# The bonus term of an RWKV-6 recurrence: from a unit of its own on VectorE to a tile made on GpSimd

## The chip, the cores and the metric

The kernel runs on one core of a Trainium2 chip. The metric is the device time in microseconds (us) of one execution, the median of several runs. Engines are named as in the profile: PE is TensorE (PEld its weight loads), DVE is VectorE, ACT is ScalarE, POOL is GpSimd, SP is SyncE, which only issues DMAs here. All data are float32.

## The reference

One RWKV-6 block on `x` of 32 sequences, 128 tokens, 512 channels (32 heads of 16). A layernorm and a token shift give five mixed inputs; four products give `r`, `k`, `v` and the gate, a small two-layer product gives the decay `w`. Then, per sequence and head, a state of 16 x 16 runs over the tokens:

```
def step(s, rkvw):
    r_t, k_t, v_t, w_t = rkvw
    a = k_t[:, :, :, None] * v_t[:, :, None, :]
    out = jnp.einsum('bhk,bhkd->bhd', r_t, u * a + s)
    return (a + w_t[:, :, :, None] * s, out)
```

The term with `u` is the bonus: the token's own `k` and `v`, weighted by `u`, which the state does not hold yet. Its sum over the 16 key channels is one number per token and head, `rk = sum_q r_q u_q k_q`, times `v`. After the recurrence come a norm per head, the gate, a product with `Wo` and the residual, then a second layernorm with a channel-mixing part (three products) and a second residual.

## The kernel before

**Groups and lanes.** The sequences are taken in NG = 8 groups of 4. In the recurrence the 128 partitions are the 4 x 32 pairs of sequence and head; `r`, `k`, `v`, `w` are tiles of 128 x 16 channels x 128 tokens, brought into this layout by DMAs (`to_lanes`).

**Tokens in pairs.** The state is computed for every second token only. `prep` (L567) multiplies neighbouring decays into `w01`, folds the decay of the second token into `k` and that of the first into `r`, and `bonus` (L627) makes two small tiles for a group: `rk` (128 x 128 tokens) and `a10` (128 x 64 pairs), the latter holding what the first token of a pair gives to the second.

**Units.** The recurrence of a group runs in two halves `dh` of 8 value channels (DH = 8), each with 16 units `q`, one per key channel (S = 16), and one more unit for the bonus. A unit goes through the engines so:

- POOL (`rec_pool`): product `am` = v x k_q (L704, 128 x 1024), then the sum of each pair into `a` (L708, 128 x 504). ACT puts the initial state into the first column of `a` (L690) and a copy of `w01` into the PSUM tile `sc` (L679).
- DVE (`rec_dve`): a scan of `sc` with `a` (L726), which runs all 64 pair steps of 8 channels in one instruction, and the product with r_q into `rm` (L728, 128 x 1024).
- PE (`rec_pe`): 8 transposes of `rm` with the permutation `by_head`, accumulated over all units in the PSUM tile `acc` (L761). After the last unit ACT copies `acc` into `y` (`rec_out`, L775).

The unit q = 16 has no scan. DVE makes `rm` = v x rk (L735), then v of the first tokens x a10 into a PSUM tile (L738), and adds that to the second tokens of `rm` (L742). PE transposes it like the others, as the 17th and last term of `acc`.

**Buffers.** `am` has 1, `a` 2, `rm` 2, `sc` 2, `acc` 1, `w01` 1, `v`, `r` and `k` 2 each, `blk` (128 x 512 in SBUF, which also takes projections on their way out) 4, `ps` (PSUM) 4, `y` 1.

**The other work.** `front_mix`, `front_proj` and `front_gate` make the inputs of later groups (products at L391 and L410; in groups after the first, part of the mixing adds are on POOL, L467), `layernorm_T` has a small power on POOL (L352). `back` does all that follows the recurrence (products at L849, L391, L923, L939). For the last group, `back` runs in two halves of two sequences, `last1` and `last2`.

**Order.** Each engine runs its instructions in the order in which the program emits them. That order is made by a small planner (`Plan`): every part of the work is a generator that yields `Op`s with an engine, an assumed duration, the buffers that it reads, writes, allocates and ends. `Plan.start` works out when an operation could start; among those that could start within `EPSILON` us of the earliest, `pick` takes the one with the smallest due value. Due values run linearly from v0 to v1 over the steps of a generator, in units of groups, from the table `DUE`. A generator whose `need` is not met, or whose buffers are all open, is passed over. So a change of EPSILON, of DUE, or of any Op can move every instruction of every engine, and with them the DMA issues on the SP and ACT queues.

Of the kernel before, what the change touches and what calls it, by code (L numbers as in the profile page):

```python
# [11 lines left out]
ALU = mybir.AluOpType  # L12
AX = mybir.AxisListType

P = 128
B, L, E = 32, 128, 512
H, S = 32, 16
# [3 lines left out]
NG = B // GB  # L21
N = GB * L
T2 = L // 2
DH = 8
# [11 lines left out]
PE, DVE, ACT, POOL, SP = range(5)  # L36
# [6 lines left out]
LANDING = 2.0  # L43
HOP = (0.2, 0.05, 0.05, 0.04, 0.08)
ON_POOL = (2, 3, 4)
EPSILON = 0.0388


DUE = {"rec": (0.171, 1.108), "mix": (-4.67, -2.417), "proj": (-4.683, 4.311), "gate": (0.588, 0.608), "prep": (-4.19, 1.684), "back": (-0.012, 3.928), "last1": (-21.388, 9.796), "last2": (10.392, 13.665)}


class Buf:
# [20 lines left out]
class Plan:  # L73
# [103 lines left out]
    def pick(self, best):  # L177
        t0 = min(t for t, _ in best)
        return min((x for x in best if x[0] <= t0 + EPSILON), key=lambda x: x[1][3] + x[1][4] * x[1][2])


@with_exitstack
def rwkv6_block(ctx: ExitStack, tc: tile.TileContext, x, prev, s0, vecs, u, maa_w1, maa_w2,
# [11 lines left out]
    nc = tc.nc  # L195
# [84 lines left out]
    def pair(ap):  # L280
        return ap.rearrange("p c (n j) -> p c n j", j=2)
# [386 lines left out]
    unit = {}  # L668
# [25 lines left out]
    def rec_pool(gs):  # L694

        for g in gs:
            d = data[g]
            yield Op(POOL, 0.0, need=lambda: "w01" in d and ("v", "all") in d)
            k, v = d["k"], d["v"]
            for dh in range(NDH):  # L700
                ds = slice(dh * DH, (dh + 1) * DH)
                for q in range(S):
                    (am,) = yield Op(POOL, 2.39, r=[(k, None), (v, None)], w=[(0, None)], alloc=["am"], port=True)
                    nc.gpsimd.tensor_tensor(am.t, v[:, ds, :], k[:, q : q + 1, :].to_broadcast([P, DH, L]), ALU.mult)  # L704
                    yield Op(POOL, 0.0, need=lambda: (g, dh, q, "a") in unit)
                    a, am2 = unit[g, dh, q, "a"], pair(am.t)
                    yield Op(POOL, 1.03, r=[(am, None)], w=[(a, 1)], port=True, end=[am])
                    nc.gpsimd.tensor_tensor(a[:, :, 1:T2], am2[:, :, 0 : T2 - 1, 0], am2[:, :, 0 : T2 - 1, 1], ALU.add)  # L708
                    unit[g, dh, q, "sum"] = True
            k.open = False  # L710

    def rec_dve(gs):

        for g in gs:
            d = data[g]
            yield Op(DVE, 0.0, need=lambda: "w01" in d and ("v", "all") in d)
            r, v = d["r"], d["v"]
            r2, v2 = pair(r.t), pair(v.t)
            for dh in range(NDH):
                ds = slice(dh * DH, (dh + 1) * DH)  # L720
                for q in range(S):
                    yield Op(DVE, 0.0, need=lambda: (g, dh, q, "sum") in unit and (g, dh, q, "sc") in unit)
                    a, sc = unit[g, dh, q, "a"], unit[g, dh, q, "sc"]
                    yield Op(DVE, 1.22, r=[(a, None)], w=[(sc, None)], end=[a])
                    scf = sc.t.rearrange("p d n -> p (d n)")
                    nc.vector.tensor_tensor_scan(scf, scf, a.t.rearrange("p d n -> p (d n)"), 0.0, ALU.mult, ALU.add)  # L726
                    (rm,) = yield Op(DVE, 1.21, r=[(sc, None), (r, None)], w=[(0, None)], alloc=["rm"], end=[sc])
                    nc.vector.tensor_tensor(  # L728
                        pair(rm.t), sc.t.unsqueeze(3).to_broadcast([P, DH, T2, 2]),
                        r2[:, q : q + 1, :, :].to_broadcast([P, DH, T2, 2]), ALU.mult)  # L730
                    unit[g, dh, q, "rm"] = rm
                q = S
                yield Op(DVE, 0.0, need=lambda: "a10" in d)
                (rm,) = yield Op(DVE, 1.2, r=[(v, None), (d["rk"], None)], w=[(0, None)], alloc=["rm"], port=True)
                nc.vector.tensor_tensor(rm.t, v[:, ds, :], d["rk"].t.unsqueeze(1).to_broadcast([P, DH, L]), ALU.mult)  # L735
                (am,) = yield Op(DVE, 0.67, r=[(v, None), (d["a10"], None)], w=[(0, None)], alloc=["ps"], port=True)
                bo = am.t.rearrange("p (d n) -> p d n", n=T2)
                nc.vector.tensor_tensor(bo, v2[:, ds, :, 0], d["a10"].t.unsqueeze(1).to_broadcast([P, DH, T2]),  # L738
                                        ALU.mult)
                yield Op(DVE, 0.67, r=[(am, None)], w=[(rm, None)], end=[am])  # L740
                rm2 = pair(rm.t)
                nc.vector.tensor_tensor(rm2[:, :, :, 1], rm2[:, :, :, 1], bo, ALU.add)  # L742
                unit[g, dh, q, "rm"] = rm
            r.open = v.open = d["rk"].open = d["a10"].open = False

    def rec_pe(gs):

        for g in gs:
            d = data[g]
            for dh in range(NDH):  # L750
                acc = None
                for q in range(S + 1):
                    yield Op(PE, 0.0, need=lambda: (g, dh, q, "rm") in unit)
                    rm = unit[g, dh, q, "rm"]
                    if acc is None:
                        (acc,) = yield Op(PE, 0.875, r=[(rm, None)], w=[(0, None)], alloc=["acc"], end=[rm])
                    else:
                        yield Op(PE, 0.875, r=[(rm, None)], w=[(acc, None)], end=[rm])
                    for i in range(DH):

                        nc.tensor.matmul(acc[:, i, :], lhsT=rm[:, i, :], rhs=by_head, is_transpose=True,  # L761
                                         start=(q == 0 and i % 4 == 0), stop=(q == S), skip_group_check=True)
                unit[g, dh, "acc"] = acc

    def rec_out(gs):
# [181 lines left out]
    for gen, n in ((rec_dve, 2), (rec_pool, 3), (rec_act, 1), (rec_state, 1), (rec_pe, 2), (rec_out, 0.1)):  # L947
        v0, v1 = DUE["rec"]
        plan.add(gen(range(NG)), v0, NG - 1 + v1, n * NU * NG)
    for g in range(NG):  # L950
        for gen, name, n in ((front_mix, "mix", 40), (front_proj, "proj", 72), (front_gate, "gate", 17),
                             (prep, "prep", 40), (back, "back", 140)):
            v0, v1 = DUE[name]
            if name != "back" or g < NG - 1:
# [4 lines left out]
    for bs, name in (((0, 1), "last1"), ((2, 3), "last2")):  # L959
        v0, v1 = DUE[name]  # L960
        plan.add(back(NG - 1, data[-1], bs, W), NG - 1 + v0, NG - 1 + v1, 130)
# [38 lines left out]
```

## Time and profile before

| | |
|---|---|
| median of 3 runs | 1536.72 us (1534.43 to 1536.81) |
| the profiled execution | 1535.0 us, of which the span from the first to the last instruction is 1533.2 us |
| mean granted PE clock | 0.959 |
| PE | 5344 matmul passes, busy 1410.0 us |
| DVE | 1618 instructions, busy 1270.9 us |
| ACT | 1277 instructions, busy 656.2 us |
| POOL | 632 instructions, busy 1024.8 us |
| DMA | 146.88 MB |

A float32 product of 512 columns shows as two passes, so 16 products of 128 x 128 x 512 are 32 entries. The busy time of a group of instructions is the union of their spans; the mean duration of a matmul is longer than its share of that union, since one begins before the one before it has drained. A line "A <- B" among the waits says that engine A was idle in front of its instruction until B released it.

### The profile page before, as it was taken

The numbers are of one execution on the slowest core, as the hardware profiler recorded it, in microseconds if no ns is written. First come the engines' busy times: TensorE is split into PE (matmuls) and PEld (weight loads), VectorE is DVE, ScalarE is ACT, GpSimd is POOL, SyncE is SP. The second block draws the span as 40 slices with busy tenths as digits, with TensorE's granted clock in tenths as the row PEclk, the third lists the DMA queues.
The fourth block names the chain that finished last, engine by engine and source line by source line (L and its number), as shares of the span: only waits on it lengthen the run. The fifth ranks groups of instructions, "written<-read, shape, count | busy, mean of one in ns | idle before, by whom it ended". The sixth has DMA issues, their size and how long they took to land.

```text
span 1533.2 us, 16578 instructions
## 1 busy us (share of the span) xinstructions
PE 1410.0 (92%) x5344; PEld 746.6 (49%) x5344; DVE 1270.9 (83%) x1618; ACT 656.2 (43%) x1277; POOL 1024.8 (67%) x632
## 2 busy tenths in 40 slices
PE   3997898899999999999999999999999998778788
PEld 1343454455554555455554555455544555455444
DVE  5537789989998899899988899899988898878732
ACT  4233242423743356323743365424733354344242
POOL 3014893877787859687786959686777959678400
PEclk9798899899999999999999999999999999889879
DMA  6120331244304431244304521343305421400220
GB/s 223 42 84 23 104 108 29 78 132 145 117 11 144 144 131 43 79 133 142 117 29 134 183 92 35 97 140 124 110 32 163 126 89 41 159 27 28 93 71 28
DMA packets 127559, 146.88 MB, mean 96 GB/s; under 512 B 8176, under 2 KB 77296, under 8 KB 126448
## 3 DMA queue, kind: packets, MB, share of 16 engines
q1 hardware_dynamic: 92112, 128.81, 25.6%
q10 hardware_dynamic: 35360, 17.02, 3.9%
q8 instruction: 42, 0.69, 0.2%
q14 instruction: 45, 0.37, 0.1%
HBM read 94.41 MB, written 17.83 MB: 73 GB/s over the span
## 4 chain that ended last, share of the span: by engine, by line
PE 51%; DVE 27%; POOL 13%; issue 6%; DMA 2%; ACT 1%; SPq 1%; DVEq 0%; POOLq 0%; ACTq 0%
PE ps L391 18%; PE acc L761 8%; POOL am L704 7%; PE ps L939 6%; PE ps L923 6%; PE ps L410 6%; DVE sc L726 5%; POOL a L708 4%; DVE rm L728 4%; PE ps L849 2%; DVE rk L642 2%; DVE ps L634 2%; PE ps L397 2%; PE ps L444 2%; DVE ps L470 1%
## 5 line engine op out<-in xcount | busy, mean ns | idle before, releaser
L704 POOL TENSOR_TENSOR am<-v,k 128x1024 f32<-128x1024 f32 x256 | 610.3, 2384 | 88.7 <-DMA r<-blk 70.4
L391 PE MATMUL ps<-mx,wt 128*128 128x512 f32 (+1 forms) x1312 | 583.2, 593 | 8.8 <-DVE mx L472 3.4
L708 POOL TENSOR_TENSOR a<-am 128x504 f32<-128x504 f32 x256 | 286.1, 1118 | 201.5 <-DVE sc L726 181.1
L391 PEld LDWEIGHTS ps<-mx,wt 128*128 128x128 f32 x1312 | 244.3, 194 | 276.2 <-issue 259.1
L728 DVE TENSOR_TENSOR rm<-sc,r 128x1024 f32<-128x1024 f32 x256 | 312.9, 1222 | 38.3 <-PE acc L761 22.9
L726 DVE TENSOR_TENSOR_SCAN sc<-sc,a 128x512 f32<-128x512 f32 x256 | 313.4, 1224 | 32.7 <-POOL a L708 30.5
L761 PE MATMUL acc<-by_head,rm 128*128 128x128 f32 x2176 | 290.8, 283 | 36.0 <-DVE rm L728 29.9
L761 PEld LDWEIGHTS acc<-by_head,rm 128*128 128x128 f32 x2176 | 252.3, 146 | 135.9 <-issue 54.4
L679 ACT COPY sc<-w 128x512 f32<-128x512 f32 x256 | 151.4, 591 | 219.5 <-DVE rm L728 197.0
L690 ACT COPY a<-st 128x8 f32<-128x8 f32 x256 | 52.2, 204 | 180.1 <-DVE sc L726 156.4
L467 POOL TENSOR_TENSOR mx<-mx,xnT 128x512 f32<-128x512 f32 x84 | 99.7, 1198 | 40.9 <-DVE mx L465 40.3
L923 PE MATMUL ps<-wt,mx 128*128 128x512 f32 x256 | 115.7, 595 | 0.0
L540 ACT COPY blk<-ps 128x512 f32<-128x512 f32 x96 | 56.0, 584 | 137.6 <-PE ps L391 137.6
L849 PE MATMUL ps<-wt,mx 128*128 128x512 f32 x256 | 112.8, 598 | 0.6 <-DVE rk L642 0.6
L410 PE MATMUL ps<-tha,w2p 64*128 64x512 f32 x256 | 89.1, 677 | 18.0 <-DVE mx L472 12.0
L939 PE MATMUL ps<-wt,ev 128*128 128x512 f32 x224 | 102.4, 600 | 2.7 <-DVE mx L472 2.7
L352 POOL TENSOR_TENSOR rstd<-rstd,mhalf 128x4 f32<-128x4 f32 (+1 forms) x17 | 20.2, 1191 | 120.1 <-DVE rstd L350 120.1
L470 DVE SCALAR_TENSOR_TENSOR ps<-ps,vec,sx 128x512 f32<-128x512 f32 x76 | 57.3, 753 | 36.7 <-PE ps L410 36.3
L465 DVE SCALAR_TENSOR_TENSOR mx<-ps,vec,sx 128x512 f32<-128x512 f32 x84 | 61.8, 743 | 21.8 <-PE ps L410 21.7
L849 PEld LDWEIGHTS ps<-wt,mx 128*128 128x128 f32 x256 | 48.9, 192 | 62.5 <-issue 56.5
L923 PEld LDWEIGHTS ps<-wt,mx 128*128 128x128 f32 x256 | 46.4, 190 | 51.0 <-issue 46.8
L939 PEld LDWEIGHTS ps<-wt,ev 128*128 128x128 f32 x224 | 40.9, 192 | 45.3 <-issue 39.9
(108 smaller groups left out, 1341.1 us busy)
## 6 DMA issues: line engine op xcount, KB each, us to landing
x<-in_x SPq DMA_DIRECT2D x15, 1024.0 KB
wt<-in_wk SPq DMA_DIRECT2D x8, 1024.0 KB
wt<-in_wr SPq DMA_DIRECT2D x8, 1024.0 KB
wt<-in_wg SPq DMA_DIRECT2D x8, 1024.0 KB
dgate<-blk SPq DMA_DIRECT2D x32, 256.0 KB
wt<-in_wo SPq DMA_DIRECT2D x8, 1024.0 KB
wt<-in_fk SPq DMA_DIRECT2D x8, 1024.0 KB
wt<-in_fr SPq DMA_DIRECT2D x8, 1024.0 KB
```

The source lines that it names most:

```text
L391: nc.tensor.matmul(p, lhsT=w[:, c, e * P : (e + 1) * P], rhs=xin[:, c, cols], start=(c == 0), stop=(c == NE - 1))
L410: nc.tensor.matmul(p.t, lhsT=w[h, :], rhs=t[h, :], start=True, stop=True)
L467: nc.gpsimd.tensor_tensor(bt(x5[:, f, :]), bt(x5[:, f, :]), row(xnT, f, 1), ALU.add)
L679: nc.scalar.copy(sc.t, d["w01"][:, q : q + 1, :].to_broadcast([P, DH, T2]))
L704: nc.gpsimd.tensor_tensor(am.t, v[:, ds, :], k[:, q : q + 1, :].to_broadcast([P, DH, L]), ALU.mult)
L708: nc.gpsimd.tensor_tensor(a[:, :, 1:T2], am2[:, :, 0 : T2 - 1, 0], am2[:, :, 0 : T2 - 1, 1], ALU.add)
L726: nc.vector.tensor_tensor_scan(scf, scf, a.t.rearrange("p d n -> p (d n)"), 0.0, ALU.mult, ALU.add)
L728: nc.vector.tensor_tensor(pair(rm.t), sc.t.unsqueeze(3).to_broadcast([P, DH, T2, 2]), r2[:, q : q + 1, :, :].to_broadcast([P, DH, T2, 2]), ...
L761: nc.tensor.matmul(acc[:, i, :], lhsT=rm[:, i, :], rhs=by_head, is_transpose=True, start=(q == 0 and i % 4 == 0), stop=(q == S), skip_grou ...
L849: nc.tensor.matmul(p.t, lhsT=att[:, c, b * L : (b + 1) * L], rhs=wot[:, c, :], start=(c == 0), stop=(c == NE - 1))
L923: nc.tensor.matmul(p.t, lhsT=xr[:, c, b * L : (b + 1) * L], rhs=frt[:, c, :], start=(c == 0), stop=(c == NE - 1))
L939: nc.tensor.matmul(p2.t, lhsT=kv[:, c, b * L : (b + 1) * L], rhs=fvt[:, c, :], start=(c == 0), stop=(c == NE - 1))
```

## The change

In groups 1 to 6 the bonus is no longer a 17th unit. POOL makes it at the end of each half, after its last sum: v x rk into an `am` tile (128 x 1024), v of the first tokens x a10 into a `blk` tile (128 x 512), and the sum of that into the second tokens of the `am` tile. DVE adds this tile to the `rm` of the last key channel (q = 15) in one instruction of 128 x 1024, and that `rm` is the last one that PE transposes for the half. The `am` tile stays in use until DVE's add has read it. Groups 0 and 7 keep the old way. EPSILON and the table DUE get other values, and DUE two keys (`warm0`, `warm1`) that no generator uses.

```
-EPSILON = 0.0388
+EPSILON = 0.0765
-DUE = {"rec": (0.171, 1.108), "mix": (-4.67, -2.417), "proj": (-4.683, 4.311), "gate": (0.588, 0.608), "prep": (-4.19, 1.684), "back": (-0.012, 3.928), "last1": (-21.388, 9.796), "last2": (10.392, 13.665)}
+DUE = {"rec": (0.054, 1.282), "mix": (-7.976, -3.297), "proj": (-5.908, 6.149), "gate": (0.501, 0.521), "prep": (-6.193, 1.057), "back": (-0.552, 4.384), "last1": (-21.31, 19.219), "warm0": (-1.403, 5.777), "warm1": (4.25, 7.453), "last2": (12.656, 20.506)}
...
 rec_pool, after the 16 units of a half:
+                if g in (0, NG - 1):
+                    continue
+
+                yield Op(POOL, 0.0, need=lambda: "a10" in d)
+                (am,) = yield Op(POOL, 2.39, r=[(d["rk"], None), (v, None)], w=[(0, None)], alloc=["am"], port=True)
+                nc.gpsimd.tensor_tensor(am.t, v[:, ds, :], d["rk"].t.unsqueeze(1).to_broadcast([P, DH, L]), ALU.mult)
+                (c,) = yield Op(POOL, 1.05, r=[(d["a10"], None), (v, None)], w=[(0, None)], alloc=["blk"], port=True)
+                cv, am2 = c.t.rearrange("p (d n) -> p d n", n=T2), pair(am.t)
+                nc.gpsimd.tensor_tensor(cv, pair(v.t)[:, ds, :, 0],
+                                        d["a10"].t.unsqueeze(1).to_broadcast([P, DH, T2]), ALU.mult)
+                yield Op(POOL, 1.05, r=[(c, None)], w=[(am, None)], port=True, end=[c])
+                nc.gpsimd.tensor_tensor(am2[:, :, :, 1], am2[:, :, :, 1], cv, ALU.add)
+                unit[g, dh, "bonus"] = am
...
 rec_dve, in the loop over q, after the product of L728:
+                    if q == S - 1 and 0 < g < NG - 1:
+                        yield Op(DVE, 0.0, need=lambda: (g, dh, "bonus") in unit)
+                        bo = unit[g, dh, "bonus"]
+                        yield Op(DVE, 1.2, r=[(bo, None)], w=[(rm, None)], port=True, end=[bo])
+                        nc.vector.tensor_tensor(rm.t, rm.t, bo.t, ALU.add)
                     unit[g, dh, q, "rm"] = rm
                 q = S
+                if 0 < g < NG - 1:
+                    continue
...
 rec_pe:
-                for q in range(S + 1):
+                last = S - 1 if 0 < g < NG - 1 else S
+                for q in range(last + 1):
...
-                                         start=(q == 0 and i % 4 == 0), stop=(q == S), skip_group_check=True)
+                                         start=(q == 0 and i % 4 == 0), stop=(q == last), skip_group_check=True)
```

## The prediction, made before the change was run

> **What bounds the kernel now.** I read the page first: shares per engine, then the chain that ended last.
>
> ```profile
> span 1533.2 us, 16578 instructions
> PE 1410.0 (92%) x5344; PEld 746.6 (49%) x5344; DVE 1270.9 (83%) x1618; ACT 656.2 (43%) x1277; POOL 1024.8 (67%) x632
> PE 51%; DVE 27%; POOL 13%; issue 6%; DMA 2%; ACT 1%; SPq 1%; DVEq 0%; POOLq 0%; ACTq 0%
> ```
>
> PE, DVE and POOL all carry much of the chain, so an average can't decide. In the chain in order of time the same pieces come back every 170.3 us (a MATMUL of L923 starts at 597.13, 767.40, 937.66 and 1107.90). So I cut the span at those points and at the end of the recurrence, and asked for the busy time of each engine per stretch (columns: length, then PE, PEld, DVE, ACT, POOL busy with counts, granted clock, DMA share).
>
> ```profile
> 767.30:937.60 170.30, 167.89 (x666) 88.75 (x666) 156.10 (x198) 80.39 (x158) 130.28 (x79) 1.00 0.33 106
> ...
> 1244.00:1437.00 193.00, 165.44 (x678) 99.82 (x677) 157.56 (x167) 82.75 (x164) 157.40 (x93) 0.92 0.20 69
> 1437.00:1533.20 96.20, 75.97 (x233) 41.89 (x231) 36.86 (x83) 34.63 (x70) 1.40 (x2) 0.86 0.21 71
> ```
>
> In the steady stretch PE works 167.9 of 170.3 us (98.6%) at full clock, DVE 156.1 (92%), POOL 130.3 (76%). Eight passes of a 512-column product take 3.44 us from start to start of the next group, 430 ns each, so the modelled ends don't mislead: PE sets the period. From 1244 on that is over: the fronts are done, and the recurrence of the last one and a half groups, then the last back part, set the end.
>
> Next, inside one period (597 to 767.3), the groups that the edit touches, and what POOL waits for:
>
> ```profile
> L735 DVE TENSOR_TENSOR rm<-v,rk 128x1024 f32<-128x1024 f32 x2 | 2.4, 1216 | 0.0
> L738 DVE TENSOR_TENSOR ps<-v,a 128x512 f32<-128x512 f32 x2 | 2.9, 1426 | 0.3 <-ACT blk L513 0.3
> L742 DVE TENSOR_TENSOR rm<-rm,ps 128x512 f32<-128x512 f32 x2 | 1.4, 683 | 0.0
> L761 PE MATMUL acc<-by_head,rm 128*128 128x128 f32 x274 | 34.9, 275 | 0.3 <-DVE rm L728 0.3
> L704 POOL TENSOR_TENSOR am<-v,k 128x1024 f32<-128x1024 f32 x33 | 78.9, 2392 | 2.3
> L467 POOL TENSOR_TENSOR mx<-mx,xnT 128x512 f32<-128x512 f32 x12 | 14.0, 1181 | 5.8 <-DVE mx L465 5.7
> POOL a L708 <- DVE sc L726: 20.0, 6, 7.3
> DVE sc L726 <- POOL a L708: 3.2, 6, 1.0
> ```
>
> POOL waits 20.0 us per period for DVE to give back an `a` buffer, DVE only 3.2 us for POOL: POOL runs ahead. The timeline says by how much: POOL's last sum of a half ends at 712.6 while DVE's scan of it starts at 732.6 (20.0 us ahead), and at 794.0 against 801.7 (7.7 us). In the last group both leads are 0.0.
>
> **What the Trainium skill says.** "SBUF — State Buffer", section "Who interferes with whom": a DVE instruction with two SBUF inputs contends with a GpSimd one that reads SBUF, and the later of them blocks until the first is done. The trace agrees: L738, two SBUF inputs, takes 0.70 us mostly and 2.15 us once per period; L735 takes 1.22 us and at worst 3.33. "GPSIMD Engine Reference", section "3.1 Elementwise — side-by-side cycle accounting" gives 4497 ns for a float32 add of two tensors of 2048 elements; L704 (1024) at 2.36 and L467 (512) at 1.18 us are in proportion, so rows of this trace price the new POOL work. "TensorE: Matmul & The Clock Gate", section "Why this matters for your kernels", says that idle gaps above some 3 us bring the PE clock down; here 1300 to 1400 us shows PE busy 75 of 100 us at clock 0.86. Idle PE thus costs more than its length.
>
> **The change, part by part.** It covers groups 1 to 6, two halves each: 12 boundaries.
>
> *PE, removed:* 8 transposes per boundary. L761 takes 34.9 us for 274, 0.127 us each, so 1.02 us per boundary, 2.04 per period, 12.2 us in all. Up to about 1244 PE is the bound, so this is on the path: group 6 counts partly, 11 boundaries certainly (11.2 us). The first of the 16 units still opens the accumulator and the last closes it; nothing else moves on PE. I take 12.2 (ends: 10 and 13).
>
> *DVE, removed and added:* out go 2.4 + 2.9 + 1.4 = 6.7 us per period, in come two adds of 128x1024 from SBUF. The nearest row is L603 (1.22 us, same shape, two SBUF inputs), so 2.4 us; bound above by 3.33 each if POOL holds the port. Net -4.2 us per period, 25 in all, beside PE's work and therefore worth nothing in the steady stretch.
>
> *POOL, added:* 2.39 + 1.18 + 1.18 = 4.75 us per boundary by L704 and L467, 9.5 per period, 57 in all. POOL goes from 130 to 140 of some 168 us. What hides it: the lead of 7.7 and 20.0 us. POOL finishes the bonus before DVE's last product of the half (2.45 us after its scan) is done. If a lead were zero, DVE would wait 4.75 - 2.45 = 2.3 us.
>
> *The new wait:* `am` has one buffer, and the bonus stays in it until DVE has added it. Queued behind on POOL: the next half's first product, its sum, any L467 and L352, and behind these DVE's next scan. Priced at the boundary of 637.8: DVE's last product ends at 637.8, the add at 639.0, then POOL's product 2.36 and sum 1.02, so the next scan could start at 642.5. In the kernel before it starts at 642.2, since DVE spends that time on L735, L738 and L742. At 735.0 the same sum gives 739.8 against 740.9. So the boundary costs nothing, but POOL's stock of two to three units is gone. Can it be done without? Between 740.9 and 801.7 DVE takes 16 units in 60.8 us; POOL needs 16 x 3.55 = 56.8. Between 642.2 and 732.6 POOL needs 56.8 + 14.0 (L467) + 2.9 (L352) = 74 of 90 us. It fits, in the second half with 4 us to spare.
>
> *Smaller parts:* one of four `ps` buffers is no longer held for L738 and L742 (about 2.8 us at a boundary); one of four `blk` buffers is held by POOL for 2.4 us instead. Opposite in sign, on 12 occasions, neither ever seen as a wait of over 0.3 us at L738: nothing, ends -1 and +2 us. No DMA is added or moved by the bonus.
>
> *The new order:* EPSILON and DUE change, so every engine's instruction order is made anew, and every DMA issue on the SP and ACT queues with it. The keys `warm0` and `warm1` name no stream that the code adds, so they do nothing. The profile can't price this. A steady stretch with 2.4 us of idle PE per period has little to win; the stretches outside (0 to 340: PE idle 59 us; 1244 to the end: 48 us) have much to win or lose. I take 0, ends -25 and +25.
>
> *The tail:* at 1304.6 DVE ends the last product of group 6. POOL's lead there is 1.5 us, so the bonus is ready 3.2 us after DVE reaches it at the most, and the add moves the first product of group 7 from 1300.6 to some 1306.6. Its first scan would start at 1310 against 1312.4 before, because L735 to L742 are out of DVE's way. I take 0, ends 0 and +6.
>
> Sum on the profiled execution (1535.0 us, span 1533.2): 1535.0 - 12.2 + 0 + 0 = 1522.8. That execution is 1.7 us below the median of 1536.7, so the median becomes 1524.5.
>
> **Rivals.**
>
> *The new order wins more.* From 1300 to 1400 and 1450 to 1500 PE is idle 37 us and its clock is down. If the new due times bring a third of that into use, 12 us come on top: about 1512. For: DUE gives the last back halves quite other spans. Against: the recurrence of group 7 is a chain of 32 units through POOL, 113 us long at the least, then 96 us of back work, and the change leaves group 7's units as they were.
>
> *Slower: the handshake over `am` makes the recurrence the bound.* With zero lead at a boundary, DVE waits 2.3 us for the bonus, adds for 1.2, waits 3.4 for product and sum: 6.9 us, less the 3.4 us of L735 to L742, so 3.5 us longer. If the new order leaves no lead at half of the boundaries and nothing to put in the gap, 6 x 3.5 = 21 us come on top and the PE gain is lost as idle PE: about 1557; at all twelve, 1579. It decides once the recurrence of a group, 170.3 us long now, can't shrink to 168.2, that is once POOL has less than the 4 us to spare worked out above. For: group 7 shows zero leads, and DVE and POOL both get close to PE. Against: the leads of 7.7 and 20.0 us.
>
> *No change.* The 2 us per period turn up as idle PE, since the order is made for other limits: 1536.7.
>
> **How the numbers follow.** About 0.2% (3 us) is what a measurement can tell from no change. My case, with PE as the bound and the order giving or taking a few us: 0.52. The order winning more: 0.20. No change: 0.06. Slower by the handshake or a worse order outside the steady stretch: 0.22. So faster 0.72, same 0.06, slower 0.22. The likeliest time is 1524.5, its own range 1514 to 1533; to hold eight in ten the range goes from 1502 to 1549.
>
> **What would show it.** Counts: PE 5248 (96 fewer), DVE 1594, POOL 668. The period falls to about 168.2 us with PE still above 98% in it; DVE busy about 152, POOL about 140 per period. The new add takes 1.2 us, not more, since POOL stands still then. POOL's wait for the add is the new long wait, and DVE's wait for POOL's sums stays below 10 us per period. Wrong, if PE falls below 97% in the steady stretch, if DVE waits for the bonus or for POOL's first sum of a half, or if the period is right and the gain is lost or doubled before 340 or after 1244.

## The result and the profile after

The changed kernel takes 1562.99 us (median of 4 runs, 1560.94 to 1563.62), the kernel before, measured beside it, 1535.83 us: a ratio of 1.0175, 95% interval 1.0158 to 1.0193. It is 27 us slower where 12 us faster were predicted. The counts of instructions are as predicted. Line numbers move: the scan is L739 now, its product L741, the new add L748, the transposes L782, the bonus on POOL L715, L718 and L721; back's products are L870, L391, L944 and L960.

First the page after (span and instructions; busy time, share and instructions of each engine; the chain that ended last by engine):

```profile
span 1559.1 us, 16445 instructions
PE 1407.2 (90%) x5248; PEld 741.3 (48%) x5248; DVE 1245.8 (80%) x1594; ACT 657.0 (42%) x1277; POOL 1072.9 (69%) x668
PE 60%; DVE 21%; POOL 11%; issue 5%; DMA 2%; ACT 2%; SPq 1%; ACTq 0%; POOLq 0%; DVEq 0%
```

PE and DVE are busy for less time than before, ACT for as long, POOL for 48 us more, in a span that is 26 us longer: what grew is waiting. One steady period, cut at the same MATMUL (now L944, at 812.94 and 989.22), by the stretches view (length, then PE, PEld, DVE, ACT, POOL busy with counts, granted clock, DMA share, GB/s):

```profile
812.94:989.20 176.26, 168.42 (x648) 88.00 (x648) 153.43 (x194) 80.56 (x157) 138.12 (x84) 0.99 0.32 103
```

176.3 us for 170.3, with PE at 95.6% and DVE at 87%: no engine is full any more. Now the waits of that period (engine and line, what it waited for: us in total, times, longest):

```profile
POOL mx L467 <- DVE mx L465: 13.0, 6, 4.1
...
POOL am L704 <- DVE rm L748: 7.3, 1, 7.3
...
DVE sc L739 <- POOL a L708: 5.9, 6, 2.6
...
DVE mx L465 <- PE ps L410: 4.2, 4, 1.3
...
PE acc L782 <- ACT xnT L367: 3.9, 1, 3.9
...
POOL a L708 <- DVE sc L739: 3.6, 2, 3.4
```

POOL's 20.0 us of waiting for an `a` buffer became 3.6, and 7.3 us of waiting for the add, so the stock is gone as predicted. DVE's wait for sums rose from 3.2 to 5.9 us and stayed under the 10 us named, and DVE never stood for the bonus itself. What nobody had on the list is PE, which stands 3.9 us in one piece.

**Where in time.** The start of the first scan of a half, after less before, in us, read from both timelines (in the kernel before these scans start at 570.6, 642.2, 812.5, 982.7, 1152.9 and 1312.4):

```
                             g2 half 1   g3     g4     g5     g6     g7    end of span
after                          -1.3     +8.5  +14.5  +20.5  +21.4  +27.6    +25.9
```

Nothing is lost up to 570; then 9.8 us within half 1 of group 2, 6.0 us in each of the next two groups, 1 and 6 us in groups 5 and 6, and the tail gives 2 us back.

**Where in the period,** from the starts of the scans of group 4 (first scan of half 0; last scan of half 0; first scan of half 1; last scan of half 1; first scan of the next group), with DVE's idle time in each piece, short gaps included, in brackets:

```
              half 0        its end     half 1       its end        period
before      90.4 (9.0)    8.3 (0.1)   60.8 (3.3)   10.8 (1.8)      170.3
after       90.3 (10.7)   7.5 (1.7)   66.4 (4.7)   12.1 (5.7)      176.3
```

DVE has 2.7 us less to do and stands 8.6 us more, 3.9 of them at the end of half 1. But 5.6 of the 6.0 us lie within half 1, where DVE stands only 1.4 us more: it has more to do there. The lines view of DVE in that piece, first before, then after (count; then busy us and mean ns):

```profile
L470 DVE SCALAR_TENSOR_TENSOR ps<-ps,vec,sx 128x512 f32<-128x512 f32 x6 | 4.5, 755 | 0.6 <-PE ps L410 0.5
L472 DVE TENSOR_TENSOR mx<-ps,xnT 128x512 f32<-128x512 f32 x6 | 4.1, 692 | 0.2
```

```profile
L470 DVE SCALAR_TENSOR_TENSOR ps<-ps,vec,sx 128x512 f32<-128x512 f32 x8 | 6.0, 750 | 0.6 <-PE ps L410 0.6
L472 DVE TENSOR_TENSOR mx<-ps,xnT 128x512 f32<-128x512 f32 x8 | 5.5, 691 | 0.3
L465 DVE SCALAR_TENSOR_TENSOR mx<-ps,vec,sx 128x512 f32<-128x512 f32 x2 | 1.4, 735 | 0.0
```

The new order puts six more instructions of the mixing, 4.3 us, between the scans of half 1. Before they stood in half 0, which has not become shorter for it, and at the end of half 1.

How the engines stand at that end is in after's timeline (start, duration, engine, line, operation, in brackets the idle time before it and what ended it):

```profile
993.81 1.02 PE L410 MATMUL ps<-tha,w2p 64*128 64x512 f32 x2
994.87 0.75 DVE L465 SCALAR_TENSOR_TENSOR mx<-ps,vec,sx 128x512 f32<-128x512 f32 x1 [1.32 <-PE ps L410]
995.68 1.12 PE L410 MATMUL ps<-tha,w2p 64*128 64x512 f32 x2 [0.84 <-DVE mx L465]
...
996.84 0.75 DVE L465 SCALAR_TENSOR_TENSOR mx<-ps,vec,sx 128x512 f32<-128x512 f32 x1 [1.22 <-PE ps L410]
997.51 1.22 DVE L748 TENSOR_TENSOR rm<-rm,am 128x1024 f32<-128x1024 f32 x1
...
997.66 2.09 POOL L467 TENSOR_TENSOR mx<-mx,xnT 128x512 f32<-128x512 f32 x1 [0.79 <-DMA w<-blk]
999.71 2.36 POOL L704 TENSOR_TENSOR am<-v,k 128x1024 f32<-128x1024 f32 x1
```

PE and DVE hand each other pieces of the mixing, each idle while the other works; then POOL's L467 takes 2.09 us instead of 1.18 beside DVE's add, and only after it comes POOL's first product of the next group.

### The profile page after: what moved, and what is told of

Its sections match the earlier page's. It is cut to its first block, busy times and chain, and to the rows that moved or that the text cites. A ratio compares the mean times of both kernels' runs of the same rounds, so it can differ in the third digit from the quotient of the medians.

```text
span 1559.1 us, 16445 instructions
## 1 busy us (share of the span) xinstructions
PE 1407.2 (90%) x5248; PEld 741.3 (48%) x5248; DVE 1245.8 (80%) x1594; ACT 657.0 (42%) x1277; POOL 1072.9 (69%) x668
## 4 chain that ended last, share of the span: by engine, by line
PE 60%; DVE 21%; POOL 11%; issue 5%; DMA 2%; ACT 2%; SPq 1%; ACTq 0%; POOLq 0%; DVEq 0%
PE ps L391 27%; PE acc L782 8%; POOL am L704 7%; PE ps L870 6%; PE ps L410 5%; PE ps L960 4%; PE ps L944 4%; DVE sc L739 4%; DVE rm L741 4%; POOL a L708 3%; DVE ps L470 2%; DVE mx L472 2%; PE ps L397 2%; PE ps L444 1%; DMA x<-in_x 1%
## 5 line engine op out<-in xcount | busy, mean ns | idle before, releaser
L391 PE MATMUL ps<-mx,wt 128*128 128x512 f32 (+1 forms) x1312 | 588.7, 597 | 7.3 <-DVE mx L472 3.6
L391 PEld LDWEIGHTS ps<-mx,wt 128*128 128x128 f32 x1312 | 246.0, 196 | 275.9 <-issue 252.0
L739 DVE TENSOR_TENSOR_SCAN sc<-sc,a 128x512 f32<-128x512 f32 x256 | 313.3, 1224 | 57.5 <-POOL a L708 56.1
L782 PE MATMUL acc<-by_head,rm 128*128 128x128 f32 x2080 | 286.7, 287 | 67.4 <-DVE rm L741 50.2
L741 DVE TENSOR_TENSOR rm<-sc,r 128x1024 f32<-128x1024 f32 x256 | 312.6, 1221 | 41.1 <-PE acc L782 27.0
L708 POOL TENSOR_TENSOR a<-am 128x504 f32<-128x504 f32 x256 | 268.6, 1049 | 95.1 <-DVE sc L739 60.7
L782 PEld LDWEIGHTS acc<-by_head,rm 128*128 128x128 f32 x2080 | 245.8, 148 | 167.5 <-DVE rm L741 70.8
L467 POOL TENSOR_TENSOR mx<-mx,xnT 128x512 f32<-128x512 f32 x84 | 111.2, 1337 | 81.9 <-DVE mx L465 78.6
L944 PE MATMUL ps<-wt,mx 128*128 128x512 f32 x256 | 116.2, 597 | 5.1 <-DVE mx L465 5.1
L870 PE MATMUL ps<-wt,mx 128*128 128x512 f32 x256 | 112.7, 597 | 0.4 <-PE ps L391 0.3
L410 PE MATMUL ps<-tha,w2p 64*128 64x512 f32 x256 | 89.0, 678 | 19.4 <-DVE mx L472 13.8
L960 PE MATMUL ps<-wt,ev 128*128 128x512 f32 x224 | 101.3, 595 | 1.6 <-DVE mx L472 1.6
L352 POOL TENSOR_TENSOR rstd<-rstd,mhalf 128x4 f32<-128x4 f32 (+1 forms) x17 | 16.6, 978 | 113.5 <-DVE rstd L350 113.2
L465 DVE SCALAR_TENSOR_TENSOR mx<-ps,vec,sx 128x512 f32<-128x512 f32 x84 | 60.8, 742 | 25.2 <-PE ps L410 25.1
L870 PEld LDWEIGHTS ps<-wt,mx 128*128 128x128 f32 x256 | 48.7, 192 | 61.6 <-issue 57.2
L944 PEld LDWEIGHTS ps<-wt,mx 128*128 128x128 f32 x256 | 46.6, 190 | 62.2 <-issue 48.8
L960 PEld LDWEIGHTS ps<-wt,ev 128*128 128x128 f32 x224 | 40.4, 190 | 43.3 <-issue 39.9
```

The source lines that it names most:

```text
L391: nc.tensor.matmul(p, lhsT=w[:, c, e * P : (e + 1) * P], rhs=xin[:, c, cols], start=(c == 0), stop=(c == NE - 1))
L410: nc.tensor.matmul(p.t, lhsT=w[h, :], rhs=t[h, :], start=True, stop=True)
L467: nc.gpsimd.tensor_tensor(bt(x5[:, f, :]), bt(x5[:, f, :]), row(xnT, f, 1), ALU.add)
L741: nc.vector.tensor_tensor(pair(rm.t), sc.t.unsqueeze(3).to_broadcast([P, DH, T2, 2]), r2[:, q : q + 1, :, :].to_broadcast([P, DH, T2, 2]), ...
L870: nc.tensor.matmul(p.t, lhsT=att[:, c, b * L : (b + 1) * L], rhs=wot[:, c, :], start=(c == 0), stop=(c == NE - 1))
L944: nc.tensor.matmul(p.t, lhsT=xr[:, c, b * L : (b + 1) * L], rhs=frt[:, c, :], start=(c == 0), stop=(c == NE - 1))
```

## The experiments

An order that is "replayed" is the recorded sequence of the planner's choices of one kernel, followed stream by stream, so that an edit changes only the operations it names. Medians in us; before took 1534.7 to 1535.5 beside these runs. The period is the distance from the first scan of a group to that of the next, in groups 3 and 4.

| run | order | bonus | median | ratio, 95% interval | period |
|---|---|---|---|---|---|
| e1 | new tables, old code | unit on DVE | 1601.1 | 1.0440 [1.0413, 1.0468] | uneven |
| e2 | old tables, new code | in `am` | 1636.9 | 1.0667 [1.0651, 1.0683] | uneven |
| r0 | before's, replayed | left out | 1531.2 | 0.9977 [0.9968, 0.9987] | 169.9 |
| r4 | before's | DVE's add only | 1534.8 | 1.0004 [0.9995, 1.0013] | 169.9 |
| r3 | before's | POOL's part only | 1549.4 | 1.0090 [1.0075, 1.0105] | 172.4 |
| r2 | before's | in `am` | 1557.1 | 1.0138 [1.0123, 1.0154] | 172.7 |
| r1 | before's | tile of its own | 1560.2 | 1.0161 [1.0146, 1.0176] | 173.6 |
| f1 | before's | own tile, half 0's after the power | 1558.8 | 1.0150 [1.0133, 1.0168] | 172.9 |
| a0 | after's, replayed | left out | 1554.8 | 1.0128 [1.0112, 1.0143] | 176.7 |
| a2 | after's | own tile | 1562.2 | 1.0177 [1.0161, 1.0194] | 177.0 |
| a4 | after's, recurrence ahead at half ends | own tile | 1579.7 | 1.0297 [1.0277, 1.0317] | 178.4 |
| a5 | after's, product first on PE | in `am` | 1569.6 | 1.0226 [1.0212, 1.0240] | 176.3 |
| a6 | a5 and DVE's add early | in `am` | 1574.8 | 1.0255 [1.0240, 1.0271] | 176.3 |
| a7 | as a5 | left out | 1570.8 | 1.0230 [1.0216, 1.0244] | 176.8 |
| a8 | after's, two loads early | in `am` | 1563.0 | 1.0181 [1.0167, 1.0195] | 176.3 |
| a10 | a5 and a8 | in `am` | 1565.7 | 1.0192 [1.0178, 1.0206] | 176.3 |
| a11 | as a10 | left out | 1561.1 | 1.0171 [1.0157, 1.0185] | 176.7 |
| b8 | before's, two loads early | unit on DVE | 1534.3 | 0.9994 [0.9986, 1.0002] | 170.3 |

### Tables and code apart: e1, e2

```
e1, kernel before:            e2, kernel after:
-EPSILON = 0.0388             -EPSILON = 0.0765
+EPSILON = 0.0765             +EPSILON = 0.0388
 and DUE likewise              and DUE likewise
```

> The kernel before with the new EPSILON and DUE alone; the bonus stays a unit of its own. If the new order is what costs the time, this kernel is slow too: 1555 to 1580 us, with a steady period of 174 us or more. If the wait for the one am buffer is what costs it, this kernel is within some 10 us of the one before (1526 to 1546), with a period near 170.3.

> The bonus on POOL with the old EPSILON and DUE. If the new order is what costs the time, 1515 to 1535 us, a period near 168.2. If the am wait costs it, 1550 to 1580 us, a period of 173 to 177, and DVE's last product of a half to the next scan takes well over the 5 us that I worked out.

Both are far slower than either kernel: 1601 and 1637 us, outside everything that was expected of them. Each crossing makes an order that neither kernel has, so it doesn't tell what a part of the change costs. Hence the replayed orders.

### What the removed work is worth: r0

```
 rec_pool: the part from "L715" to "L721" gone
 rec_dve:  the add gone, no unit q = 16 in groups 1 to 6
 rec_pe:   16 units in groups 1 to 6
```

> Every engine keeps the order of the kernel before, written out; the bonus of groups 1 to 6 is left out altogether (no L735, L738, L742, no 17th unit, nothing in their place). This prices what is removed. If PE is the bound as the prediction has it: 2.0 us per period less, about 1522 to 1526 us. If PE's 98.6% was not the bound, less than half of that: 1530 to 1537.

All that the change takes off PE and DVE is gone here, and nothing is put in its place: 0.23% less, some 3.5 us (by the interval 2.0 to 4.9), where the prediction had 12.2. Per period, again by the stretches view:

```profile
639.60:809.40 169.80, 166.16 (x650) 86.85 (x649) 149.86 (x192) 80.19 (x157) 128.93 (x78) 1.00 0.32 107
```

PE works 1.7 us less than before, DVE 6.2 us less, and the period shrinks by 0.4. Its pieces are 92.0, 8.1, 60.7 and 9.1 us: the end of half 1 gives 1.7 us and half 0 takes 1.6 of it back. That PE alone doesn't set the period stands in the kernel before too. The chain that ended last, in order of time (start, us, what), leaves PE at the end of half 0 for 33 us of DVE's work:

```profile
876.57 6.88 PE ps L849 x16
883.57 1.31 DVE x L858 x4
...
915.41 1.24 DVE rm L728
916.69 1.09 PE acc L761 x8
```

A period earlier it runs through DVE and POOL from 667 to 746. So paths through several engines are about as long as PE's own.

### One part at a time in before's order: r4, r3, r2, r1, f1

```
r4: r0, and DVE adds v to the last product (no POOL part; not the bonus)
r3: r0, and POOL makes the bonus in a tile "bo" of its own that nobody adds
r2: the bonus made in "am" and added: the change without its order (POOL's next product
    comes after DVE's add, and so after the power L352 where that stood behind it)
r1: as r2, but  alloc=["bo"]  for  alloc=["am"]  ("bo" is bf16, so that it fits)
f1: as r1, with half 0's bonus behind the power L352 in POOL's order
```

> As the run without a bonus in the order of before, but DVE adds v to the last product of each half in groups 1 to 6, in place of the bonus (which is left out). It prices DVE's 1.2 us alone: 1531 to 1534 us if DVE has room for it, 1540 or more, up to 12 x 1.2 = 15 us over the run without, if DVE and PE are in line at that place. If POOL holds the port, the add takes up to 3.5 us instead of 1.22.

> As the last one, but DVE does not add the tile (the bonus of groups 1 to 6 is left out of the result). It prices POOL's three instructions alone, without any wait for or by them: within 2 us of the run without a bonus (1529 to 1534) if POOL's time is covered by its lead; 1540 or more if POOL's time is what the recurrence feels.

> The bonus on POOL, its tile in the one am buffer as in the changed kernel, every engine in the order of the kernel before; only where POOL's next product must wait for am is it put off until after DVE's add, past the small powers of L352. If the am wait costs nothing (the prediction's arithmetic at the boundary), 1522 to 1528 us. If the handshake costs by itself, 5 us per period or more: 1550 to 1575. If only the new order costs, as with no cost.

> As the run with the bonus in the order of the kernel before, but the bonus has a tile of its own (bfloat16, since only 2 KB per partition are left), so POOL's next product needn't wait for DVE's add and L352 stays where it was. If it is the hold on am that costs, most of the 26 us between that run and the one without a bonus go: 1531 to 1540 us, POOL's leads at the half ends again 7 and 20 us and its first product starting right after the bonus. If POOL's added 4.8 us per boundary cost by themselves, 1550 to 1558.

> As the run with the tile of its own in the order of before, but in the first half of a group POOL makes the bonus after the small power of L352 that stands next in its queue, not ahead of it. If the power that waits behind 4.8 us of bonus is what costs in that run (DVE stood 3.2 us for it per period), the period goes from 173.6 to about 170.5 and the time to 1533 to 1545 us. If it is POOL's work as such, or DVE's blocked port, the time stays at 1553 to 1562.

Over r0, by the ratios times 1535 us: DVE's add alone costs 4 us, POOL's part alone 17, both with the hold on `am` 25, both without it 28. So **POOL's part is not free**, though its lead was never used up: in r3 POOL's last sum of a half still ends 23.6 and 8.4 us ahead of DVE's scan of it. One way to the loss is in r3's timeline, POOL's share at the end of half 0 (L409 there is the power that was L352):

```profile
889.93 2.36 POOL L772 TENSOR_TENSOR bo<-v,rk 128x1024 bf16<-128x1024 f32 x1
892.25 1.75 POOL L775 TENSOR_TENSOR blk<-v,a 128x512 f32<-128x512 f32 x1
894.07 1.27 POOL L778 TENSOR_TENSOR bo<-bo,blk 128x512 bf16<-128x512 bf16 x1
895.30 2.35 POOL L761 TENSOR_TENSOR am<-v,k 128x1024 f32<-128x1024 f32 x1
897.73 1.03 POOL L765 TENSOR_TENSOR a<-am 128x504 f32<-128x504 f32 x1
898.84 2.67 POOL L761 TENSOR_TENSOR am<-v,k 128x1024 f32<-128x1024 f32 x1
901.47 1.01 POOL L409 TENSOR_TENSOR rstd<-rstd,mhalf 128x4 f32<-128x4 f32 x1
```

and DVE's at the same time:

```profile
897.24 0.44 DVE L407 TENSOR_SCALAR rstd<-mv 128x4 f32<-128x4 f32 x1
...
902.52 0.16 DVE L411 SCALAR_TENSOR_TENSOR nb<-mv,rstd 128x4 f32<-128x4 f32 x1 [3.20 <-POOL rstd L409]
```

DVE's operand for the power is there at 897.7; POOL, pushed back by 5.4 us of bonus, comes to it at 901.5, and DVE stands 3.2 us for 512 numbers. POOL is in order: its stock of sums helps the recurrence only, not the layernorm that stands in the same queue. In r3 this wait is most of what half 0 loses: 3.6 us over r0, with DVE idle 3.2 us more. f1 takes the wait away and gains only 1.4 us over r1 (1560.2 to 1558.8), less than the measurement tells: DVE's busy time rises by 2.5 us in its place (156.4 to 158.9 per period), as the bonus now runs beside other instructions of DVE. How much of the 17 us each way accounts for was not measured.

The second way is the shared port. The new add, in r1 (minimum, median, maximum in ns; then first and last start):

```profile
L805 DVE TENSOR_TENSOR rm<-rm,bo x12: 2217/2928/3346, 398.6 to 1334.3; 128x1024 f32<-128x1024 f32 x12
```

and in r2:

```profile
L805 DVE TENSOR_TENSOR rm<-rm,am x12: 1215/1226/1227, 394.4 to 1321.9; 128x1024 f32<-128x1024 f32 x12
...
  POOL am L761: 94.8, 12
```

With `am` held, POOL has nothing to do (it waits 94.8 us in all for the 12 adds) and DVE's add takes 1.22 us. Without the hold POOL runs on, and the same add takes 2.9 us, nearly the 3.35 us of the L735, L738 and L742 that it replaces. The bfloat16 tile is not the reason: a2 adds the same tile in 1.21 to 1.23 us in six of its twelve adds. The choice is between a wait and a port, and both lose: the 95% intervals of r1 and r2 (1.0146 to 1.0176, 1.0123 to 1.0154) just overlap, so the tile of its own is at best no better.

### The new order: a0, a2

```
a0: after's order replayed, the bonus left out as in r0
a2: after's order replayed,  alloc=["bo"]  for  alloc=["am"]
```

> Every engine keeps the order of the changed kernel, written out, and the bonus of groups 1 to 6 is left out (neither POOL's three instructions nor DVE's add). If the wait for am costs the time in the changed kernel too, it goes: 1530 to 1540 us, period below 172. If the changed order itself, which puts POOL's first product of a half behind L467 and DVE's next scan behind that, holds the time, it stays at 1550 to 1563, period 174 or more.

> Every engine in the order of the changed kernel, but the bonus in a bfloat16 tile of its own, so that POOL's next product does not wait for DVE's add. If the wait for am itself costs in the changed kernel, faster than it by 8 us or more: below 1555. If the order that was made around this wait holds the time, within 4 us of the changed kernel: 1559 to 1567.

The order alone, without any bonus, loses 23.6 us against before's order without the bonus (1554.8 to 1531.2). In it the bonus costs only 8 us more. The two costs cover each other (by the medians): 25.9 for the bonus and then 5.9 for the order, or 23.6 for the order and then 8.2 for the bonus, 31.8 us over r0 either way. In the steady period the bonus costs nothing in the new order (176.3 us with it, 176.7 without); what it does cost comes outside the steady periods. And a2 differs from the changed kernel by less than 1 us: lifting the hold on `am` gains nothing here. Most of its adds in the first halves take 2.0 us or more instead of 1.22, so a wait is again exchanged for a port.

### Is PE's stand the cause? a4 to a11, b8

The likeliest cause in after's timeline was PE at the end of half 0:

```profile
922.81 1.07 PE L377 MATMUL ps<-ident,ev 128*128 128x128 f32 x8
...
927.83 1.06 PE L782 MATMUL acc<-by_head,rm 128*128 128x128 f32 x8 [3.95 <-ACT xnT L367]
...
928.73 5.29 PE L391 MATMUL ps<-mx,wt 128*128 128x512 f32 x8
```

PE stands 3.95 us in front of the first transposes of half 1 (their product L741 ends at 927.69; ACT's L367, which the profile names, at 927.76, so that the two can't be told apart), and then the eight passes of L391 take 5.29 us instead of 3.60: the granted clock falls to 0.67 over 927.8 to 933. Together 5.6 us, nearly the 6.0 by which the period grew. So the next runs move what stands in the queues, with after's own order around it:

```
a4:  a2, and at half ends the next half's first sums (POOL) and first scan (DVE) moved ahead
a5:  on PE, the next L391 ahead of the first transposes of half 1
a6:  a5, and DVE's add right behind its product at the end of half 1
a8:  on SP, the loads of in_fk and in_fr ahead of the first gate store, not behind the third
a10: a5 and a8;   a7, a11: a5 and a10 with the bonus left out
b8:  a8's edit in the kernel before
```

> As the last one, but at each half end of groups 1 to 6 POOL's first products and sums of the next half stand ahead of the adds of L467 (and of L352), and DVE's first scan and product stand ahead of the additions from PSUM of the back part (L949, L951) that wait for PE. Nothing else is moved. If the changed kernel loses its time at the half ends (9.6 us from the last product to the next scan against 4.4 before, DVE idle for 5 to 6 of them), this gives back at least half of it: 1540 to 1552, period below 174. If the loss lies elsewhere, 1557 or more.

> The changed kernel with its own order and its own held tile; only in the six middle groups, at the end of the first half, the eight transposes of the second half's first unit stand on PE behind the next product of 8 passes (L391) and not ahead of it. If PE's stand of some 4 us ahead of these transposes and the halved clock after it (together some 5.8 us of the period) are what the new order loses: period 170 to 172 us, clock 1.00 after the half end, and 1530 to 1545 us. If DVE and POOL set this stretch anyway and PE's stand only shows it: the stand moves on to the next unit, 1557 us or more.

> As the one with the product first, and at the end of the second half DVE's add stands straight behind its product, ahead of two L465. If the hold on the tile at the second half end costs what its 9.6 us against 4.4 us say: some 3 us per period less than with the product first alone, 10 to 20 us in all. If the wait only moves to the projection's passes (L410 and L465, whose turn comes later on DVE): no difference, within 3 us.

> The same order as the one with the product first, with the bonus of groups 1 to 6 left out on POOL and on DVE (the result lacks it). The new order without the bonus took 1554.79 us. If PE's place for the first unit is what makes the new order worse: 1530 to 1540 us, close to the 1531.21 us of the old order without the bonus. If the order is worse in other places too: above 1545 us.

> The changed kernel with its own order and its own held tile; only the loads of the weights in_fk and in_fr stand on SP ahead of the first of a group's four gate stores and not behind the third. With the product first alone, PE went on standing 4 us: the product's weights came 5.5 to 6 us after their load was issued, and the load stood on SP behind a store that waits for DVE. Here PE's queue still has the transposes of the second half's first unit ahead of that product. If both the place on PE and the load end the stand at the same time: no gain, 1558 to 1566 us. If the load alone sets it: the stand goes, 1535 to 1550 us.

> Both edits: the loads early on SP, and the product ahead of the second half's first transposes on PE. If these two together make PE's stand: the stand of 4 us at the first half end goes, the period falls by 3 to 6 us, 1535 to 1550 us in all. If the product's own operand (the fourth quarter of mx, made by DVE behind the scan and the product of the next half) is as late: 1557 us or more.

> Both edits in the changed kernel's order with the bonus of groups 1 to 6 left out on POOL and DVE (the result lacks it). The new order without the bonus took 1554.79 us, the old one 1531.21. If loads and the product's place are what the new order loses: 1530 to 1540 us. If not: above 1548 us.

> The kernel before, its order unchanged but for the loads of in_fk and in_fr, which stand ahead of the first gate store and not behind the second. There PE has a product and some 3 us of transposes between the load's issue and its first use, about 9 us against a load of 5.5 to 6 us, so the load has slack: within 3 us of before, 1532 to 1538 us. If loads are late there too: 1525 us or less.

a4 does what it was made for: the end of half 0 takes 4.5 us and the end of half 1 7.6, with 2.6 us of DVE's idle time there instead of 5.7. But half 0 grows to 96.0 us and half 1 to 70.3 to 70.8, the period is 178.4 and the whole 17 us longer than a2. So the long half ends are not what holds the period either.

In a5 the product waited as long as the transposes had: it started at 928.61, 5.75 us after the load of its weights was issued at 922.86, and that load stands on SP behind a gate store whose data come from DVE. (The profile names DVE's product L741 there; a10, which differs from a5 in the loads alone, shows that it was the load.) In a8 the load is early, but the transposes are still in front. In a10 both are out of the way (L450 is L391 there, L841 the transposes):

```profile
927.57 1.07 PE L436 MATMUL ps<-ident,ev 128*128 128x128 f32 x8
929.47 3.02 PE L450 MATMUL ps<-mx,wt 128*128 128x512 f32 x6 [0.82 <-DVE mx L952]
934.92 1.13 PE L450 MATMUL ps<-mx,wt 128*128 128x512 f32 x2 [2.43 <-DVE mx L952]
935.88 1.04 PE L841 MATMUL acc<-by_head,rm 128*128 128x128 f32 x8
```

```profile
828.20:1004.50 176.30, 167.64 (x649) 87.27 (x648) 153.74 (x193) 80.65 (x156) 138.14 (x86) 1.00 0.32 103
929.40:935.00 5.60, 3.10 (x7) 1.06 (x7) 5.01 (x7) 5.26 (x9) 5.37 (x4) 1.00 0.00 0
758.00:763.30 5.30, 4.05 (x17) 3.15 (x18) 5.27 (x8) 3.89 (x8) 5.07 (x4) 0.68 0.31 65
```

The long stand is gone and the clock stays at 1.00, and the period is 176.30 us against 176.26. In the period before it the clock does fall at the same place (the last line), and that period takes 176.3 us as well: the clock costs nothing here. The idle time has only moved: PE now waits for the last quarter of `mx`, which DVE makes behind the new half's scan and product. The start of half 1's scans tells why nothing was won. In after, the second, third and sixteenth scan come 3.54, 9.79 and 66.38 us behind the first; in a5 3.54, 9.80 and 66.40; in a10 3.55, 9.81 and 66.40 (in before 2.96, 6.68 and 60.81). So DVE's recurrence never waited for these PE instructions: **PE's stand is a symptom**, and the theory that its removal would give some 20 to 30 us fell. a6 freed `am` earlier at the other half end and kept the period too (its whole time is 5 us longer than a5's), so that release does not set it either. a7 and a11 say the same without the bonus. b8 shows no difference in the kernel before (0.9994, interval 0.9986 to 1.0002): PE has other work there until the weights are in.

Outside the steady periods a5, a6 and a7 lose something of their own in groups 5 and 6, a10 and a11 in group 6, and the whole time of a4, a5 and a6 is longer than after's. In a6 and a7 PE stands 9.5 and 9.3 us for the load of in_fk there; the others were not followed up. None of the runs that compute the whole result beats the kernel before by more than the measurement tells.

**What stays open.** Which ring of waits holds the new order's period at 176.3 us. It is not PE's place or clock at the end of half 0, and not the loads of in_fk and in_fr. It is not the hold on `am` alone (a2), though the chain of a10 runs through that hold at the end of half 0. And it is not DVE's idle time at the end of half 1, the longest there (5.2 to 5.7 us in after, a2, a6 and a10, 6.5 in a0, 2.6 in r0), where PE's L410 and DVE's L465 wait for each other: a4 cuts it to 2.6. What is left points into half 1, where DVE has the six more instructions. The chains without the bonus, r0 first, then a0, show where it goes back from DVE to PE (`acc` is the transposes):

```profile
911.42 1.13 DVE rm L785
912.56 1.15 DVE sc L783
913.73 1.24 DVE rm L785
915.01 1.09 PE acc L821 x8
```

```profile
931.45 2.06 DVE mx L946 x3
...
941.08 1.24 DVE rm L787
942.36 1.09 PE acc L823 x8
```

In r0 that is after the product of half 1's second unit, 9.2 us after the chain left PE for DVE and ACT (but for four small transposes). In a0 it is after that of the fifth, 23.7 us after, with the mixing of the part behind the recurrence (L946, L905 in after) ahead of the third scan. This is read from the traces; no run moved these instructions back, so the cause stays open.

## Why the prediction was wrong, point by point

- **PE's 12.2 us on the path: the term that was too large.** r0 measured 3.5 us. The step that failed is "PE sets the period", taken from 98.6% busy. With PE relieved by 1.7 us per period and nothing put in place of that work, the period gave 0.4, and PE's idle time rose from 2.4 to 3.6 us: it stands for DVE five times, 0.5 to 0.8 us each. The share of a whole period was taken for the bound of each of its pieces; the chain of the kernel before, which leaves PE for 33 and 80 us of two periods, already spoke against it.
- **DVE's 4.2 us "worth nothing": right.** r4 puts 4.5 us per period of work back on DVE (149.9 to 154.4, its adds alone), and the period stays at r0's 169.9; the whole time grows by 4 us, outside the steady periods.
- **POOL's 57 us hidden by the lead: a step that turns the sign by itself in the old order.** r3 measured 17 us for it, with leads of 23.6 and 8.4 us intact. The lead was the wrong measure: it covers the recurrence, not the small power in the same queue, and it says nothing of the port. The prediction named L352 behind the new wait and put no price on it.
- **The boundary "costs nothing": nearly right in the old order, for which the sum was made.** From the last scan of a half to the next scan r2 takes 9.0 and 10.5 us, where before takes 8.3 and 10.8. In the new order it is 7.5 and 12.1; at the second end L465 and L467 stand in between, and the sum left out what else is in the queues.
- **The add at 1.2 us: right** (1.218 us, median of 12), but the reason only in part: in the second halves of groups 1 to 4 POOL doesn't stand still, its L467 starts beside the add and is the one that takes longer (2.09 us at 997.66). And r1 shows that the hold is the add's price.
- **The new order at 0, ends -25 and +25: a term put at nothing, and the largest single one; the ends held.** a0 against r0 says +23.6 us, enough to turn the sign without the bonus. The prediction looked for it outside the steady stretch; by the first scan of group 5, a0 is already 22.0 us behind r0.
- **The tail at 0: about right,** 2 us were given back from group 7 on.
- **The rival of the handshake** gave 1557 us, close to the measured time, but that is luck, since its mechanism did not show: in groups 3 to 5 POOL is 19.3 and 9.8 us ahead at the half ends where the rival supposed no lead, DVE never stands for the bonus, and a2 without the handshake is as slow.
- **The sign to watch** did its work: PE fell below 97% in the steady stretch, and that was named as what would make the prediction wrong.

## What to carry to other kernels

When three engines are all above three quarters busy, take the work off first and put nothing in its place (r0): that one run bounds what the move can win in the old order, here 3.5 us instead of 12. A new order is a change of its own: run it without the added work as well (a0). Price work that goes to GpSimd by what stands behind it in its queue and by DVE's two-input instructions beside it, not by its idle time or its lead. And a long stand of the busiest engine, even one as long as the loss, is a cause only if taking it away moves the instructions of the others.

## What was new about the hardware

- A DVE add of 128 x 1024 from two SBUF tiles took 1.22 us with GpSimd standing (r2) and 2.2 to 3.3 us beside a GpSimd product (r1; in r4 1.23 us in the five that found it standing, 1.35 to 3.35 in the seven others). The Trainium skill, "SBUF — State Buffer", section "Who interferes with whom", says that the two contend; here a tiny one stands too: in f1 DVE's L411 (128 x 4) takes 0.16 us in the median, and 2.31 us at 899.05, where POOL's bonus runs beside it.
- After a stand of 3.95 us PE's clock was halved for some 3.4 us (worked out from the granted clock of 0.67 over 5.2 us; passes every 0.85 us instead of 0.43), in the middle of a stretch that is over 95% busy. The Trainium skill, "TensorE: Matmul & The Clock Gate", section "Why this matters for your kernels", warns of gaps above some 3 us. Here shorter ones went with a lower clock too, and not each time: a10's gaps of 0.8 and 2.4 us went with 0.68 over 5.3 us at 758, and the same gaps a group later left it at 1.00; in a0 a gap of 1.92 us at 570.8 stands at the start of 10 us at 0.66. So these traces show no fixed length of a gap. It cost no time in a10, where both periods take 176.3 us.
- A weight load of 1 MB, issued right behind gate stores of 0.25 MB and just ahead of a second load of 1 MB, was followed by its first use 5.5 to 6.0 us after its issue, wherever PE stood and the profile names that load (in a5, a6 and a7).
